# Last stage of a two-layer scan and expert kernel: norms of two chunks loaded with the first chunk's, and third expert layers three pairs behind the first two

## The chip, the cores and the metric

The kernel runs on one core of one Trainium2 chip. The metric is the device time of one execution in microseconds. The time of the kernel before is the median of three runs. A separate execution was recorded by the profiler; it gives the span and the trace, and its times are counted from the start of its span.

## The reference, cut to what matters

A tensor x of 2 batches, 256 channels and 64 x 64 positions goes through a first state-space block, a second bidirectional one, and a soft mixture of 8 experts. The change touches the mixture alone:

```python
def _L1_ffn_ref(x, Wr, br, W1, b1, g1, be1, m1, v1, W2, b2, g2, be2, m2, v2, Wo, bo):
    feat = jnp.mean(x, axis=0)                       # over the two batches
    w = jax.nn.softmax(feat @ Wr + br, axis=-1)      # per position, over 8 experts
    h = jax.nn.relu(_bn(jnp.einsum('bfd,edh->bfeh', x, W1) + b1, g1, be1, m1, v1))
    h = jax.nn.relu(_bn(jnp.einsum('bfeh,ehk->bfek', h, W2) + b2, g2, be2, m2, v2))
    y = jnp.einsum('bfeh,ehd->bfed', h, Wo) + bo
    return jnp.einsum('bfed,fe->bfd', y, w)

t = t + _L1_ffn_ref(_ln_t(t), ...)                   # t: 2 batches x 4096 positions x 256
```

## The kernel before, in words

Channels lie on the 128 partitions, in KC = 2 halves; the 4096 positions are cut into 8 chunks of T = 512. All is float32. A tile of a chunk is 128 x 1024, 512 KB.

A long first stage runs the scans of both state-space blocks for both batches. Beside them it computes as many experts as fit, for 74 of the 128 combinations of batch, chunk and expert. Of these it stores the third layer's product, not yet weighted by the softmax, in DRAM (`u_dram`). It also stores most normalised chunks in `nf_dram`.

The last stage, which the change touches, does the remaining 54 combinations, called pairs here, and sums everything up. Chunk 7 is done for all experts in both batches (`whole`). Chunks 6 to 0 (`rest`, in this order) have batch 1 left: 6 experts of chunk 6, and 8 experts each of chunks 5 to 0.

The steps for a chunk i, with the names by which the trace lists them:

- `load_n` loads the norms n of both batches (L1086, two DMAs of 512 KB in the queue of GpSimd).
- `both` adds the batches to nm on GpSimd (L1108); `logits` multiplies it by Wr on TensorE (lt, L1115) and takes the softmax over experts on VectorE (L1120 to L1134) with an exponential on ScalarE (L1130).
- `spread` transposes the softmax on TensorE (wt, L1140), copies it on ScalarE (wts, L1142), writes it to DRAM (w_dram, L1144) and reads it back to all partitions (wb, L1146, 2048 KB). Both DMAs are in GpSimd's queue. wb has two buffers.
- `load_x` loads the residual x of both batches (L1156, in SP's queue); `bias` multiplies the softmax by bo on TensorE (bi, L1163), copies it on ScalarE (L1164) and adds it to both x on GpSimd (L1166).
- `add_early` loads one early product u (L1170, SP's queue, three buffers), multiplies it by its weight (L1171) and adds it to x (L1172), both on VectorE.
- `layer` computes the first and the second layer of a pair: for each half two products on TensorE (hp, L1201), then a relu with scale and offset on ScalarE (h, L1205). `weigh` multiplies the second layer's h by the softmax weight on VectorE (L1212). `last_layer` adds the third layer's products to y in PSUM (L1220); after the chunk's last pair VectorE adds y to x (L1225) and `store` writes x out (L1175, SP's queue).

The loop over the pairs gives the order of the work, and no scheduler changes it: `in_order` chains each engine's instructions in the order in which they were emitted. In a pair's turn come its weights' loads, its two layers, the weighting of the pair before it, the third layer of the pair two before it, and then a share of the chunk's `side` work. The list `side` of a chunk interleaves its own sums with the routes (`load_n` to `spread`) of a chunk to come, and for chunk 6 with those of chunks 7 and 5; chunk 5's list also has chunk 7's sums. Chunk 6's side work begins in its third pair's turn. As each queue is in order, a waiting instruction holds what stands behind it in its queue.

Of the kernel before, what the change touches and what calls it, by code (L numbers as in the profile page):

```python
# [42 lines left out]
F32 = mybir.dt.float32  # L43
# [4 lines left out]
P = 128  # L48
NB, C, L = 2, 256, 4096
KC = C // P  # L50
T = 512
# [80 lines left out]
def hybrid_kernel(ctx: ExitStack, tc: tile.TileContext, a: dict, out: bass.AP):  # L132
# [49 lines left out]
    def over_channels(t):  # L182
        return t.rearrange("p (o t) -> p o t", o=1).to_broadcast([P, KC, T])


    with ExitStack() as st:
# [121 lines left out]
        )  # L308
        kinds = [(l0, 256, 0, False), (lf, 512, 1, False), (lb, 512, 1, True)]
        jobs = [Scan(p, d, b, layer, flip) for b in range(NB) for p, d, layer, flip in kinds]  # L310
        steps = [(job, c) for job in jobs for c in range(NCH)]
        starts = [sum(8 * job.nj for job, _ in steps[:i]) for i in range(len(steps) + 1)]
# [698 lines left out]
        for g in range(nq):  # L1011
            i, jp, n = quads[g]
# [49 lines left out]
    with ExitStack() as st:  # L1062
        mw = st.enter_context(tc.tile_pool(name="mw", bufs=1))
        mk = st.enter_context(tc.tile_pool(name="mk", bufs=2))
# [3 lines left out]
        n, x, y, acc, wts, wb, lt, w_dram = {}, {}, {}, {}, {}, {}, {}, {}  # L1068
# [5 lines left out]
        rest, whole = [], []  # L1074
# [2 lines left out]

        def load_n(i):

            for b in range(NB):  # L1080
                n[b, i] = mk.tile([P, KC, T], F32, tag="n", name=f"n_{i}{b}", bufs=6)
                if (b, i) in featured:
                    src = nf_dram[b][:, i, :, :]
                else:
                    src = t_dram[b][:, :, i * T : (i + 1) * T]
                nc.gpsimd.dma_start(n[b, i], src)  # L1086

        def layer_norm(i):
            for b in range(NB):
                if (b, i) in featured:  # L1090
                    continue
                v = n[b, i]
                mean = psp.tile([P, T], F32, tag="ps", name=f"mean_m{i}{b}")
                for k in range(KC):
                    nc.tensor.matmul(mean, mean_w, v[:, k, :], start=(k == 0), stop=(k == KC - 1))
                nc.vector.tensor_tensor(v, v, over_channels(mean), ALU.subtract)
                sq = mk.tile([P, KC, T], F32, tag="u", name=f"sq_{i}{b}", bufs=3)
                nc.scalar.activation(sq, v, AF.Square)
                var = psp.tile([P, T], F32, tag="ps", name=f"var_m{i}{b}")
                for k in range(KC):  # L1100
                    nc.tensor.matmul(var, mean_w, sq[:, k, :], start=(k == 0), stop=(k == KC - 1))
                r = mk.tile([P, T], F32, tag="r", name=f"r_{i}{b}", bufs=1)
                rsqrt(r, var, eps5)
                nc.vector.tensor_tensor(v, v, over_channels(r), ALU.mult)

        def both(i):
            n["sum", i] = mk.tile([P, KC, T], F32, tag="nm", name=f"nm_{i}", bufs=1)
            nc.gpsimd.tensor_tensor(n["sum", i], n[0, i], n[1, i], ALU.add)  # L1108

        def logits(i):  # L1110

            lt = psp.tile([P, q, E], F32, tag="ps", name=f"lt_{i}")
            for t in range(q):
                for k in range(KC):
                    nc.tensor.matmul(  # L1115
                        lt[:, t, :], n["sum", i][:, k, t * P : (t + 1) * P], wr[:, k, :],
                        start=(k == 0), stop=(k == KC - 1),
                    )
            w = n["w", i] = mk.tile([P, q, E], F32, tag="w", name=f"w_{i}")
            nc.vector.tensor_tensor(  # L1120
                w, lt, br.rearrange("p (o e) -> p o e", o=1).to_broadcast([P, q, E]), ALU.add
            )
            mx = mk.tile([P, q], F32, tag="mx", name=f"mx_{i}")
            nc.vector.tensor_reduce(mx, w, AX.X, ALU.max)

            def over_experts(v):
                return v.rearrange("p (q o) -> p q o", o=1).to_broadcast([P, q, E])

            nc.vector.tensor_tensor(w, w, over_experts(mx), ALU.subtract)
            nc.scalar.activation(w, w, AF.Exp)  # L1130
            sm = mk.tile([P, q], F32, tag="sm", name=f"sm_{i}")
            nc.vector.tensor_reduce(sm, w, AX.X, ALU.add)
            nc.vector.reciprocal(sm, sm)
            nc.vector.tensor_tensor(w, w, over_experts(sm), ALU.mult)  # L1134

        def spread(i):

            pt = psp.tile([P, T], F32, tag="ps", name=f"wt_{i}")
            for t in range(q):
                nc.tensor.transpose(pt[:E, t * P : (t + 1) * P], n["w", i][:, t, :], ident)  # L1140
            wts[i] = mk.tile([E, T], F32, tag="wt", name=f"wts_{i}", bufs=3)
            nc.scalar.copy(wts[i], pt[:E, :])  # L1142
            w_dram = drp.tile([E, T], F32, name=f"w_dram{i}")
            nc.gpsimd.dma_start(w_dram, wts[i])  # L1144
            wb[i] = mk.tile([P, E, T], F32, tag="wb", name=f"wb_{i}")
            nc.gpsimd.dma_start(  # L1146
                wb[i], w_dram.rearrange("e (o t) -> o e t", o=1).to_broadcast([P, E, T])
            )

        def routes(i):  # L1150
            return [lambda: load_n(i), lambda: layer_norm(i), lambda: both(i), lambda: logits(i), lambda: spread(i)]
# [40 lines left out]
        def load_w(name, e):  # L1192
            we[name, e] = mw.tile([P, KC, C], F32, name=f"{name}_{e}")
            nc.sync.dma_start(we[name, e], a[name][e].rearrange("(k p) n -> p k n", p=P))

        def layer(x, l, e, tag):
            h = mk.tile([P, KC, T], F32, tag=f"h{l}", name=f"h{l}_{tag}", bufs=2 + l)
            for m in range(KC):
                ps = psp.tile([P, T], F32, tag="ps", name=f"hp{l}_{tag}_{m}")
                for k in range(KC):  # L1200
                    nc.tensor.matmul(  # L1201
                        ps, we[f"W{l + 1}", e][:, k, m * P : (m + 1) * P], x[:, k, :],
                        start=(k == 0), stop=(k == KC - 1),
                    )
                nc.scalar.activation(  # L1205
                    h[:, m, :], ps, AF.Relu,
                    bias=of[:, l, e, m : m + 1], scale=sc[:, l, e, m : m + 1],
                )
            return h

        def weigh(b, i, e, h):
            nc.vector.tensor_tensor(h, h, over_channels(wb[i][:, e, :]), ALU.mult)  # L1212

        def last_layer(b, i, e, h):
            begins, ends = (e == [p[2] for p in pairs if p[:2] == (b, i)][k] for k in (0, -1))
            if begins:
                y[b, i] = ps_o.tile([P, KC, T], F32, tag="y", name=f"y_{i}{b}")
            for m in range(KC):
                for k in range(KC):
                    nc.tensor.matmul(  # L1220
                        y[b, i][:, m, :], we["Wo", e][:, k, m * P : (m + 1) * P], h[:, k, :],
                        start=(begins and k == 0), stop=(ends and k == KC - 1),
                    )
            if ends:
                nc.vector.tensor_tensor(x[b, i], y[b, i], x[b, i], ALU.add)  # L1225
                store(b, i)
# [8 lines left out]
        for at, i in enumerate(rest):  # L1235
# [9 lines left out]
            while now or ahead:  # L1245
                work += ahead[:1] + now[:every]
                ahead, now = ahead[1:], now[every:]

        load_n(rest[0])
        for name, e in [("W1", order[0]), ("W2", order[0]), ("W1", order[1]), ("W2", order[1])]:  # L1250
            load_w(name, e)
        nc.sync.dma_start(bo, a["bo"])
        layer_norm(rest[0])
        both(rest[0])
        weights = [("Wo", order[0])]
        for k in range(2, E):
            weights += [("W1", order[k]), ("W2", order[k]), ("Wo", order[k - 1])]
# [2 lines left out]
        waiting = []  # L1260
        done = {i: 0 for i in rest}
        count = {i: sum(p[1] == i for p in pairs) for i in rest}
        for at, (b, i, e) in enumerate(pairs):
            for name, k in weights[: 6 if at else 4]:
                load_w(name, k)
            weights = weights[6 if at else 4 :]
            h = layer(n[b, i], 0, e, f"{i}_{e}_{b}")
            h = layer(h, 1, e, f"{i}_{e}_{b}")
            if at == 0:
                logits(i)  # L1270
            elif at == 1:
                spread(i)
            if waiting:
                weigh(*waiting[-1])
            waiting.append((b, i, e, h))
            if len(waiting) > 2:
                last_layer(*waiting.pop(0))
            done[i] += 1
            work = side[i] if at > 1 else []
            upto = -(-len(work) // (count[i] - done[i] + 1))  # L1280
            for fn in work[:upto]:
                fn()
            side[i] = side[i][upto:]
# [107 lines left out]
```

## Time and profile before

| what | value |
|---|---|
| median of 3 runs | 5206.82 us (5206.63 to 5207.61) |
| the profiled execution | 5213.06 us |
| its span | 5211.3 us |
| busy: PE (TensorE), DVE (VectorE), ACT (ScalarE), POOL (GpSimd) | 4298.0, 4584.8, 3681.8, 4410.2 us |
| last product of the first stage ends | 4541.8 us |
| first hp product of the last stage | 4555.17 us |
| first hp product of chunk 4 | 4748.47 us |
| busy in the last stage's L1201, L1220 on PE | 408.3, 198.0 us |
| idle before them | 15.8, 14.5 us |

PE, DVE, ACT and POOL are the four computing engines; SPq is the queue of SyncE, which only issues DMAs here. A row of the timeline gives the start in us, the duration, the engine, the line, the operation, the tiles written and read, their shapes, how many instructions the row merges, and in brackets the engine's idle time before it with what ended it. Each float32 product of the program shows as two matmul records. A row of the chain of waits gives start, duration and work: the chain is followed back from the last instruction, at each step to what released it. A row of stretches gives the stretch and its length, then busy us and number of instructions for PE, the weight loads PEld, DVE, ACT and POOL, then the granted clock of TensorE as a share of full speed, the mean busy share of the 16 DMA engines, and GB/s.

### The profile page before, as it was taken

What the parts mean: (1) busy time and instruction counts of PE and PEld (TensorE: products, weight loads), DVE (VectorE), ACT (ScalarE), POOL (GpSimd) and SP (SyncE); (2) the same over time, 40 slices, a digit from 0 to 9 for tenths busy, and PEclk for the clock granted to TensorE, in tenths of its full rate; (3) what the DMA queues carried; (4) which work ended last, traced back from release to release, by engine and by line L of the source; (5) the groups of instructions that cost most, each with busy time, mean ns of one, the idle gap of its engine ahead of it and who ended that gap; (6) DMA issues with size and microseconds to landing.
All of it is one profiled execution on the core that took longest, in us unless ns stands there. A gap on an engine that the chain in (4) does not pass through costs nothing. (4 is left out here: it accounts for less than half of the span.)

```text
span 5211.3 us, 47295 instructions
## 1 busy us (share of the span) xinstructions
PE 4298.0 (82%) x14920; PEld 1488.2 (29%) x14920; DVE 4584.8 (88%) x3083; ACT 3681.8 (71%) x7462; POOL 4410.2 (85%) x1438
## 2 busy tenths in 40 slices
PE   5777666766668888888888888888999989689999
PEld 1222212222222333332222332322333333234444
DVE  6998999999999999998989999999999999746333
ACT  5777777777767888887887888788788888522332
POOL 5998999999999999998989999999999999611010
PEclk8778888888889999999999999999999999899999
DMA  4444433344434554555555544445544455354322
GB/s 175 146 165 164 162 134 126 130 156 148 140 135 159 187 186 166 181 174 185 197 177 182 178 169 169 164 159 194 184 171 163 163 184 178 115 194 154 111 103 77
DMA packets 314731, 834.47 MB, mean 160 GB/s; under 512 B 35240, under 2 KB 102064, under 8 KB 272496
## 3 DMA queue, kind: packets, MB, share of 16 engines
q1 hardware_dynamic: 310768, 806.15, 44.5%
q0 software_dynamic: 3712, 25.30, 1.2%
q8 instruction: 118, 1.93, 0.1%
q14 instruction: 133, 1.09, 0.1%
HBM read 647.18 MB, written 184.16 MB: 160 GB/s over the span
## 5 line engine op out<-in xcount | busy, mean ns | idle before, releaser
L654 POOL TENSOR_TENSOR bq<-rxdt,bc 128x2048 f32<-128x2048 f32 x640 | 2892.9, 4542 | 34.8 <-issue 17.4
L664 ACT ACTIVATE da<-rdt,w_a 128x512 f32<-128x512 f32 x2560 | 1756.8, 686 | 113.6 <-DVE bq L690 67.8
L690 DVE TENSOR_TENSOR_SCAN da<-da,h_state,bq 128x1024 f32<-128x1024 f32 x664 | 1559.5, 2349 | 38.7 <-ACT da L664 27.3
L715 POOL TENSOR_TENSOR bq<-bq,bc 128x2048 f32<-128x2048 f32 (+1 forms) x280 | 1179.6, 4213 | 22.5
L723 PE MATMUL y<-bq,stack 128*32 128x512 f32 x5120 | 779.4, 687 | 362.1 <-POOL bq L715 337.2
L690 DVE TENSOR_TENSOR_SCAN bq<-da,h_state,bq 128x1024 f32<-128x1024 f32 x456 | 1052.3, 2337 | 27.9 <-ACT da L664 27.8
L699 DVE TENSOR_TENSOR bq<-da,bc 128x1024 f32<-128x1024 f32 x760 | 928.2, 1221 | 18.7
L912 PE MATMUL e<-eh,ew 128*128 128x512 f32 x1184 | 582.4, 621 | 60.5 <-DVE sp L513 20.5
L709 ACT COPY h_state<-da 128x2 f32<-128x2 f32 x759 | 119.3, 157 | 687.5 <-DVE bq L699 685.4
L675 ACT ACTIVATE bq<-h_state,bq,a 128x1 f32<-128x1 f32 x1120 | 429.9, 384 | 0.5
L723 PEld LDWEIGHTS y<-bq,stack 128*32 128x32 f32 x5120 | 144.9, 118 | 935.1 <-POOL bq L715 458.6
L1205 ACT ACTIVATE h<-hp,of,sc 128x512 f32<-128x512 f32 x216 | 167.7, 777 | 345.0 <-PE hp L1201 328.5
L414 PE MATMUL xs<-nx,w_in 128*128 128x512 f32 x640 | 320.1, 630 | 36.8 <-DVE xc L466 20.7
L414 PE MATMUL z<-nx,w_in 128*128 128x512 f32 x640 | 326.2, 638 | 23.7 <-DVE sp L513 16.9
L912 PEld LDWEIGHTS e<-eh,ew 128*128 128x128 f32 x1184 | 212.4, 193 | 422.3 <-issue 194.5
L912 PE MATMUL e<-en,ew 128*128 128x512 f32 x592 | 290.5, 622 | 47.3 <-DVE fcen L809 21.5
L452 PE MATMUL conv<-xs,w_conv 64*64 64x512 f32 x2560 | 320.5, 608 | 4.6 <-DVE sp L513 3.7
L761 PE MATMUL o<-sz,w_out 128*128 128x512 f32 x640 | 306.7, 620 | 0.0
L923 ACT ACTIVATE eh<-e,of,sc 128x512 f32<-128x512 f32 x296 | 223.7, 769 | 37.9 <-PE e L912 36.7
L517 POOL TENSOR_TENSOR xdt<-sp,xc 128x512 f32<-128x512 f32 x160 | 203.4, 1275 | 53.3 <-DVE sp L513 53.3
L501 PE MATMUL dt<-dbc,w_dt 64*128 64x512 f32 x320 | 197.2, 701 | 44.5 <-ACT dbc L488 27.7
L730 PE MATMUL y<-xc,w_d 128*128 128x512 f32 x320 | 181.0, 649 | 60.8 <-DVE sz L742 51.3
(138 smaller groups left out, 5043.0 us busy)
## 6 DMA issues: line engine op xcount, KB each, us to landing
rxdt<-xdtd SPq DMA_DIRECT2D x160, 1024.0 KB, 6.4
rdt<-dtd SPq DMA_DIRECT2D x160, 1024.0 KB, 6.3
bc<-bcd SPq DMA_DIRECT2D x384, 256.0 KB, 3.2
dtd<-sp SPq DMA_DIRECT2D x160, 256.0 KB, 3.5
xdtd<-xdt SPq DMA_DIRECT2D x160, 256.0 KB, 3.4
ew<-in_W SPq DMA_DIRECT2D x148, 256.0 KB, 4.8
u<-eu SPq DMA_DIRECT2D x74, 512.0 KB, 3.5
u<-u SPq DMA_DIRECT2D x74, 512.0 KB, 4.0
```

Source lines behind the costliest of these rows:

```text
L414: nc.tensor.matmul(ps, job.w["in", half][:, k, j * P : (j + 1) * P], rhs, start=(k == 0), stop=(k == KC - 1),)
L452: nc.tensor.matmul(v[r][64 * col : 64 * col + 64, :], job.w["conv"][rows, 2 * jp + j, k, :], ck["xs", jp][rows, j, k : k + T] if k < 4 els ...
L654: nc.gpsimd.tensor_tensor(bq[g], ck["rxdt", j], over_groups(ck["bc", 0, sg]), ALU.mult)
L664: nc.scalar.activation(da[g, h][:, k, :], cks[i]["rdt", j][:, q, :], AF.Exp, scale=steps[i][0].w["a"][:, j, q * SG + sg : q * SG + sg + 1],)
L675: nc.scalar.activation(bq[g][:, q, 0:1], job.h[:, j, sg, q : q + 1], AF.Identity, scale=cks[i]["a0", j][:, h, sg : sg + 1], bias=bq[g][:, ...
L690: nc.vector.tensor_tensor_scan(b if on_pool(g, h) else d, d, b, job.h[:, j, sg, 2 * h : 2 * h + 1] if c else 0.0, ALU.mult, ALU.add,)
L699: nc.vector.tensor_tensor(bq[g][:, two, :], d, cks[i]["bc", 1, sg].rearrange("p (o t) -> p o t", o=1).to_broadcast([P, 2, T]), ALU.mult,)
L715: nc.gpsimd.tensor_tensor(b, b, cks[i]["bc", 1, sg].rearrange("p (o t) -> p o t", o=1).to_broadcast([P, groups, T]), ALU.mult,)
L723: nc.tensor.matmul(y[i, j][q * CG : (q + 1) * CG, :], stack, bq[g][:, q, :], start=False, stop=(sg == SG - 1),)
L761: nc.tensor.matmul(v[m], job.w["out"][:, j, m * P : (m + 1) * P], ck["sz", j], start=False, stop=(j == job.nj - 1),)
L912: nc.tensor.matmul(ps, ew[l][:, k, m * P : (m + 1) * P], key[x][:, k, :], start=(k == 0), stop=(k == KC - 1),)
L923: nc.scalar.activation(key[dst][:, m, :], key["ps", l, m], AF.Relu, bias=of[:, l, e, m : m + 1], scale=sc[:, l, e, m : m + 1],)
```

## The change

`load_n` returns at once when a chunk's norms are loaded already. It is called for chunks 7 and 5 ahead of the loop, right after chunk 6's nm; their routes' own calls then do nothing. The second layers' h gets four buffers instead of three. The third layer of a pair is emitted in the turn of the pair three after it, not two. The weighting is left out in the turns of pairs 0 and 1; pair 0's comes in turn 2, those of pairs 1 and 2 in turn 3, and from turn 4 on again that of the pair before. At the end, three third layers are left for after the loop instead of two.

```diff
         def load_n(i):
 
+            if (0, i) in n:
+                return
             for b in range(NB):
                 n[b, i] = mk.tile([P, KC, T], F32, tag="n", name=f"n_{i}{b}", bufs=6)
...
         def layer(x, l, e, tag):
-            h = mk.tile([P, KC, T], F32, tag=f"h{l}", name=f"h{l}_{tag}", bufs=2 + l)
+            h = mk.tile([P, KC, T], F32, tag=f"h{l}", name=f"h{l}_{tag}", bufs=2 + 2 * l)
...
         layer_norm(rest[0])
         both(rest[0])
+        for i in whole[:1] + rest[1:2]:
+            load_n(i)
         weights = [("Wo", order[0])]
...
-            if waiting:
-                weigh(*waiting[-1])
+
+            for p in {0: [], 1: [], 2: waiting[:1], 3: waiting[1:]}.get(at, waiting[-1:]):
+                weigh(*p)
             waiting.append((b, i, e, h))
-            if len(waiting) > 2:
+            if len(waiting) > 3:
                 last_layer(*waiting.pop(0))
```

## The prediction

> **What bounds the kernel now.** I first cut the trace into stretches of time. The last stage's first multiplication starts at 4555.17 us. Up to 4748.47, where chunk 4's first layer begins, TensorE is busy 167 of 193 us; from there to the end it is busy 454.6 of 457.5.
>
> ```profile
> 4555.17:4748.47 193.30, 167.46 (x412) 74.40 (x413) 108.33 (x104) 49.33 (x69) 31.62 (x22) 0.93 0.55 194
> 4748.47:5206.00 457.53, 454.56 (x1086) 195.20 (x1084) 169.96 (x156) 138.79 (x184) 46.05 (x32) 1.00 0.29 103
> ```
>
> So only the first 193 us can be shortened. TensorE's rows in the timeline show each gap there, with its releaser in brackets:
>
> ```profile
> 4588.27 5.79 PE L1220 MATMUL y<-h,Wo 128*128 128x512 f32 x8 [7.61 <-DVE h L1212]
> ...
> 4610.08 1.02 PE L1140 MATMUL wt<-ident,w 128*8 128x128 f32 x4 [1.65 <-DVE w L1134]
> ...
> 4630.33 3.58 PE L1115 MATMUL lt<-wr,nm 128*128 128x8 f32 x16 [7.66 <-POOL nm L1108]
> ...
> 4691.19 5.40 PE L1220 MATMUL y<-h,Wo 128*128 128x512 f32 x8 [3.64 <-DVE h L1212]
> ...
> 4707.01 3.70 PE L1220 MATMUL y<-h,Wo 128*128 128x512 f32 x8 [3.28 <-DVE h L1212]
> ...
> 4741.06 3.70 PE L1201 MATMUL hp<-h,W 128*128 128x512 f32 x8 [1.87 <-ACT h L1205]
> ```
>
> The gaps are 25.7 us together. The blocks after them are also longer than an undisturbed one: 5.79 against 3.60, 1.02 + 4.64 against 0.60 + 3.60, 3.58 + 5.22 against 1.85 + 3.60, 5.40 and 3.70 against 3.60, 8.9 us in all. The prize is 34.6 us.
>
> The third view is the chain of waits. From 4659 to 4741 TensorE isn't on it. VectorE adds the early experts' products, and in between the queue SP waits for a finished output before it starts the next loads:
>
> ```profile
> 4690.02 0.39 SPq L1175
> 4690.47 5.59 DMA u<-u
> 4696.08 1.24 DVE u L1171
> ...
> 4715.31 1.23 DVE x L1172
> 4716.56 0.39 SPq L1175
> ...
> 4718.44 6.22 DMA u<-u
> 4724.68 3.26 DVE u L1171
> ...
> 4738.31 1.23 DVE x L1172
> 4740.25 0.77 ACT h L1205
> ```
>
> The reader should see a second bound close behind the gaps: this serial chain, not TensorE, decides when 4741 comes.
>
> **What the Trainium skill says.** "PSUM — Partial Sum Buffer", Engine vs sequencer instructions: the queues of ScalarE, VectorE and GpSimd are strict FIFO. The trace agrees: GpSimd's nm of chunk 7 (4601.29) follows its bias adds (4596.67), and ScalarE's layer at 4740.25 sits behind the softmax's exponential at 4740.12. "SBUF — State Buffer", SBUF: two separate sides: a VectorE operation with two SBUF inputs and a GpSimd one take a shared port in turn, each for its whole length. It agrees: L1172 takes 3.36 us at 4599.05 beside GpSimd, 1.22 alone. "DMA: Bandwidth & Descriptors", Issuing engines are not separate DMA queues: SP's and GpSimd's transfers share the same 16 engines, so loading earlier moves traffic and adds no bandwidth. "TensorE: Matmul & The Clock Gate", Part 1: idleness lowers the array's clock, about 3.4 us of work restores it; the longer blocks above agree roughly (3.64 us idle cost 1.8, 3.28 cost 0.1).
>
> **The change, part by part.** Call chunk 6's pairs p0 to p5 and chunk 5's q0 to q7. Undisturbed steps from start to start, by the timeline: first layer 3.43 (3.5 after lt or bi), second 3.71, y 3.43, lt 1.70, wt 0.43, bi 1.91.
>
> *Two chunks' norms early.* Four 512 KB loads go into GpSimd's queue after nm of chunk 6, so at 4557.6; chunk 7's were issued at 4578.1 and chunk 5's at 4614.65. Their issue (4 x 0.54) fills idle GpSimd time before w_dram at 4574.63, and the later issues go. They compete with the weights: 2.1 MB at the 321 GB/s of 4555 to 4588 is 6.5 us of traffic, but half of it ran beside wb (4577.60 to 4586.97) before. The weights of p0 to p2 were issued earlier than the loads; those of p3 have until 4582. Bounds for wb's landing: the fastest landing of a wb is 8.2 against 9.4, so -1 us, and +6.5 if all 2.1 MB stand ahead of w_dram. I take 0, since one 1 MB load leaves its company as another enters. Benefit: the lt of chunk 5 no longer waits at 4630.33 (7.66 and 3.3 of slow blocks).
>
> *Third layers three behind.* No instruction is added; one more h buffer is held. p0's y now stands behind p3's layers. p0 to p2 end at 4580.5, bi ends at 4582.4, p3 at 4589.6. wb lands at 4587.0; p0's weighting then overlaps GpSimd's bias adds and nm (bi start + 2.68, for 8 us, thus 4583.2 to 4591.2) and takes some 3.4: about 4590.4. The 7.6 us gap becomes 0.8. Behind that weighting on VectorE stand u_0's add, p1's and p2's weighting and the softmax: 4590.4 + 0.8 + 1.2 + 2.3 gives about 4595. lt of chunk 7 runs 4593.9 to 4595.6, its softmax starts at 4595.8, so the wt gap stays (1.7, and 1.4 slow).
>
> From there: wt 4597.4, p4 4598.2, p1's y 4602.7 + 3.7 = 4606.4, lt of chunk 5 4609.8 (nm: GpSimd after wb's issue at 4601.4, by 4605, in time), p5 4611.5. VectorE's softmax comes about a microsecond late and holds ScalarE 0.4. wt 4622.5, q0 **4622.9**; before, 4646.4. Then p3's y and bi of chunk 7 at **4633.5** (before 4657.08).
>
> VectorE after p4: u_7 ends 4620.4, the output and loads cost 5.5 as before (4641.44 to 4646.91), two adds and p5's weighting end about 4632. That releases chunk 5's wb, queued on GpSimd ahead of the bias adds; it lands near 4643. The bias adds start 2.68 after bi, 4636.2, and before q0's weighting there are 10.44 us as before (4659.76 to 4670.20): **4646.6**.
>
> *What moves on VectorE and SP.* x += y of chunk 6 (L1225) and its store stood before u_3 of chunk 7; SP's loads queued behind that store, and VectorE idled 5.37 (ending 4677.93). Now both come after u_7. There SP waits for that output anyway: u_3 to u_7 and q1's weighting run without a stall, 4647.8 to 4661; y of chunk 6 ended at 4656.7; x += y ends at 4662.1, SP's two outputs and a load cost 6.5, first add of batch 1 **4668.6** (before 4696.08: 27.5 earlier). Everything from there to chunk 4's softmax is one chain and keeps this 27.5: u_7 4689, output, loads of chunk 5's x (4694.7 for its bias add), exponential 4740.12 - 27.5 = **4712.7**, q7's second layer 4713.6.
>
> TensorE without waiting: q3's y at 4697.5 ends at 4701.0; lt waits for nm until 4702.7 and ends 4704.5, q7's first layer 4708. It is then idle 5.6 us: the gap of 1.87 has grown, because it is behind VectorE's chain. A gap of that length costs some 1.6 more (between the 0.1 and 2.2 seen). q7's second layer, q4's y, wt; chunk 4 begins at 4721.0 + 1.6 = **4722.6**, 25.9 earlier. But at this point one y fewer has been done: 3.43 comes back later. Net 22.4.
>
> *The rest.* From chunk 4 on there are 8 or 10 adds per 87 us of TensorE work, so VectorE catches up: chunk 5's last y ends 4755, its store and the load follow, first add about 4761, some 13 us later against TensorE than before, against which each y has gained 10.57 of slack; VectorE, busy 56 of 130 us in this chunk before, makes up the rest within it.  At the end three y follow one another after the last layer instead of two; the last weighting (2 us) is hidden, and TensorE's total is equal. I cost these at 0 (0 to 3 if the softmax of chunk 3 is reached late).
>
> Sum: 22.4 us of the profiled execution, 5213.1 (span 5211.3) to 5190.7. The median of the runs is 6.2 below the profiled one, and nothing suggests that those 6 us lie in this stage: 5206.8 - 22.4 = **5184**.
>
> **Rivals.**
> *A, TensorE paces:* the loads or outputs on SP cost less and VectorE's chain isn't the last. Left are 0.8 and 3.1 of gaps: 34.6 - 3.9 = 30.7, **5176**. For it: VectorE is busy only 108 of 193. Against: three SP round trips in series remain.
> *B, wb late:* w_dram and wb stand behind the early loads in GpSimd's queue: +6.5 for everything after p3, and a cold restart of 2.2: 13.7 gained, **5193**. For it: those engines were 91% busy from 4555 to 4588. Against: a dip to 45 GB/s at 4577.
> *C, no change:* VectorE's chain after bi takes up the lead (its adds wait for bi and SP, not for norms): **5203**. Against: the chain begins with TensorE's bi, which comes 23.6 earlier.
> *D, slower:* VectorE begins its adds earlier, beside more traffic, and its u loads have three buffers. A load is hidden while it lands within two adds, 4.8 us; the median is 4.4 and the longest 9.3. 29 adds lie before chunk 4's softmax; if each three wait for a 9.3 landing, 29/3 x 4.5 = 43.5 are lost: 5206.8 - 22.4 + 43.5 = **5228**. It decides from 7.1 us on (29/3 x 2.3 = 22.4). Against: after 4588 the DMA share is 0.33 to 0.55.
>
> **Chances.** Forecast 0.64, A 0.13, B 0.13, C 0.06, D 0.04. The range, 5175 to 5195, takes in A and B with their bounds and leaves C and D out. A measurement of this kernel tells about 0.2%, 10 us, from no change. Faster: forecast, A and nearly all of B, 0.88; same: C and the rest of B, 0.08; slower: D, 0.04.
>
> **What would show it.** Right: no gap at lt of chunk 5; p0's y waits under 2 us; the wt gap stays; q0's first layer about 67.8 us after the stage's first multiplication (before 91.2); a gap of 4 to 7 us before q7's second layer, behind chunk 4's exponential; none after. Wrong: wb landing over 3 us later after its issue; VectorE waiting over 7 us for any u; gaps after chunk 4 begins.

## The result and the profile after

The changed kernel takes 5189.31 us in the median of 6 runs (5187.39 to 5190.60), the kernel before 5207.22 (6 runs): ratio 0.9963, 95% interval 0.9951 to 0.9974, or 13.5 to 25.5 us. The forecast was 5184, the range 5175 to 5195. One of the later runs of the kernel before took 6108 us at a granted clock of 0.658 against some 0.92 in all others; it is left out of every figure.

The profiled execution has a span of 5188.1 us. In its `kernel.py` the lines of the last stage stand two lower, so hp is L1203, y L1222, u and x L1173 and L1174, the store L1177. First the two stretches again, each from the start of the same operation as before; the second goes to 5188.00 here, where the span ends, and went to 5206.00 of 5211.3 before:

```profile
4552.65:4721.86 169.21, 162.83 (x405) 72.14 (x405) 109.76 (x105) 49.11 (x69) 31.58 (x22) 0.94 0.63 222
4721.86:5188.00 466.14, 458.00 (x1094) 196.72 (x1092) 161.49 (x155) 138.72 (x184) 43.12 (x32) 1.00 0.29 102
```

The first stretch went from 193.3 to 169.2 us and TensorE's idle time in it from 26 to 6. It did 7 fewer matmul records there by this trace and has 8 more in the second stretch: one pair's y, which has moved behind this point. Taken to the end of the span, the second stretch grew by that y alone, from 462.8 to 466.2 us. From the first product to the end of the span the last stage took 656.1 us before (5211.3 - 4555.17) and takes 635.4 now (5188.1 - 4552.65): **20.7 us less**. I call this the stage's length and use it below, because the first stage, which no edit touches, varies by as much as some of the edits bring.

TensorE's gaps in the timeline, with the blocks behind them:

```profile
4595.09 1.02 PE L1142 MATMUL wt<-ident,w 128*8 128x128 f32 x4 [2.38 <-DVE w L1136]
4595.90 5.95 PE L1203 MATMUL hp<-n,W 128*128 128x512 f32 x8
...
4614.81 3.70 PE L1203 MATMUL hp<-h,W 128*128 128x512 f32 x8 [0.60 <-ACT h L1207]
...
4701.88 2.57 PE L1117 MATMUL lt<-wr,nm 128*128 128x8 f32 x16 [1.24 <-POOL nm L1110]
4704.29 6.43 PE L1203 MATMUL hp<-n,W 128*128 128x512 f32 x8
4712.75 5.40 PE L1203 MATMUL hp<-h,W 128*128 128x512 f32 x8 [2.03 <-ACT h L1207]
```

The reader should see which rows of before have no successor here: no y waits any more (7.61, 3.64 and 3.28 before), and the lt of chunk 5 doesn't wait for nm (7.66). The wt gap stayed. The end of the stretch, at lt of chunk 4 and q7's second layer, now waits more than before. The chain of waits says for what:

```profile
4661.50 0.39 SPq L1177
...
4661.94 0.46 SPq L1177
...
4662.45 5.46 DMA u<-u
4667.93 1.24 DVE u L1173
...
4688.41 0.39 SPq L1177
...
4690.29 6.08 DMA u<-u
4696.39 3.23 DVE u L1173
...
4711.94 0.77 ACT h L1207
4712.75 5.40 PE hp L1203 x8
```

It is the chain that was shown for before, its first add after the store (4667.93) 1.9 us later in the stage than forecast: finished output, SP's store, the loads queued behind it, VectorE's adds, the softmax, ScalarE, TensorE.

### The profile page after: what moved, and what is told of

Its sections match the earlier page's. It is cut to its first block, busy times and chain, and to the rows that moved or that the text cites. A ratio compares the mean times of both kernels' runs of the same rounds, so it can differ in the third digit from the quotient of the medians.

```text
span 5188.1 us, 47283 instructions
## 1 busy us (share of the span) xinstructions
PE 4301.2 (83%) x14920; PEld 1485.8 (29%) x14920; DVE 4576.1 (88%) x3083; ACT 3681.7 (71%) x7462; POOL 4407.2 (85%) x1438
```

## The experiments

The stages' lengths, each from its own trace (span less the start of the first hp product). The fifth column ends where chunk 4's first layer begins, the sixth is explained below:

| kernel | first product | span | stage | to chunk 4 | var_m and layer |
|---|---|---|---|---|---|
| before | 4555.17 | 5211.3 | 656.1 | 193.30 | 7.01 |
| before, second trace | 4557.17 | 5212.0 | 654.8 | 192.02 | 6.95 |
| changed | 4552.65 | 5188.1 | 635.4 | 169.21 | 6.95 |
| loads alone | 4554.39 | 5200.4 | 646.0 | 184.82 | 5.38 |
| lag alone | 4548.95 | 5195.5 | 646.6 | 182.00 | 5.38 |
| later stores | 4549.42 | 5175.2 | 625.8 | 160.05 | 6.94 |
| later transpose | 4554.37 | 5188.7 | 634.3 | 168.02 | 6.95 |
| both of these | 4559.62 | 5182.4 | 622.8 | 158.53 | 5.37 |
| weighting as before | 4548.16 | 5181.6 | 633.4 | 168.85 | 5.37 |
| chunk 5's loads alone | 4551.22 | 5186.1 | 634.9 | 168.62 | 6.95 |

The last column is one place far behind the start of chunk 4: var_m, TensorE's product for the variance in the norms of one late chunk, and the first layer after it, from var_m's start to the start of the second layer. TensorE waits 2.40 us before it in all ten traces, and yet the two blocks took 5.4 us in four of them and 6.9 to 7.0 in six. These are the rows of the changed kernel and of "weighting as before":

```profile
5016.27 3.05 PE L1103 MATMUL var_m<-sq,mean_w 128*128 128x512 f32 x4 [2.40 <-ACT sq L1100]
5019.12 4.26 PE L1203 MATMUL hp<-n,W 128*128 128x512 f32 x8
```

```profile
5011.43 1.98 PE L1103 MATMUL var_m<-sq,mean_w 128*128 128x512 f32 x4 [2.40 <-ACT sq L1100]
5013.25 3.60 PE L1203 MATMUL hp<-n,W 128*128 128x512 f32 x8
```

The granted clock over these blocks was 0.75 in the first and 1.00 in the second. This difference of 1.6 us doesn't follow the edits (the kernel before and the changed kernel both have the long blocks), and it is in the stage's length; so where an edit is worth only a few us, the column to chunk 4 says more. Each kernel but the one before has one trace, and that one's two traces differ by 1.3 us to chunk 4.

**Early loads alone.** From the kernel before:

```diff
         def load_n(i):
+            if (0, i) in n:
+                return
...
+        for i in whole[:1] + rest[1:2]:
+            load_n(i)
         weights = [("Wo", order[0])]
```

> Early loads alone, third layers two behind as before. Theory (the two halves take away different gaps, so they add up): the first y still waits for wb, 7 to 9 us plus 2 of slow blocks, the lt of chunk 5 no longer waits for nm (11 us with its slow blocks), chunk 4's first layer begins some 10 us earlier after the stage's first product than before (183 instead of 193.3): 5197. Rival (the early loads do everything, the lag nothing): 5189. Rival (the loads push wb back and give nothing by themselves): 5207.

Measured: ratio 0.9983 (0.9976 to 0.9990), 5201.9 against 5211.2 of the kernel before on the same chip; the stage is 10.1 us shorter than before, 8.5 of it ahead of chunk 4, which begins 184.8 us after the first product. TensorE's gaps at y in this kernel's timeline:

```profile
4588.31 5.40 PE L1222 MATMUL y<-h,Wo 128*128 128x512 f32 x8 [8.42 <-DVE h L1214]
...
4681.40 6.63 PE L1222 MATMUL y<-h,Wo 128*128 128x512 f32 x8 [3.78 <-DVE h L1214]
...
4697.89 5.23 PE L1222 MATMUL y<-h,Wo 128*128 128x512 f32 x8 [2.71 <-DVE h L1214]
```

All three waits at y are still there; lt of chunk 5 runs without one. The loads alone give roughly half.

**Third layers three behind alone.** The changed kernel less its two lines ahead of the loop:

```diff
-        for i in whole[:1] + rest[1:2]:
-            load_n(i)
```

> Third layers three behind alone, norms of chunks 7 and 5 loaded where they were. Theory: no gap at the first y, but lt of chunk 5 waits some 9 us for nm, because its loads stand behind wb of chunk 7; VectorE's u_3 no longer waits behind a store. Chunk 4 begins about 180 us after the first product, of which 3.4 come back at the end: 5197. Rival (the lag does everything): 5189. Rival (the gap only moves from y to lt): 5205.

Measured: ratio 0.9982 (0.9973 to 0.9990), 5200.9 against 5211.2; stage 9.6 us shorter than before. TensorE's two largest gaps:

```profile
4612.73 3.58 PE L1117 MATMUL lt<-wr,nm 128*128 128x8 f32 x16 [7.49 <-POOL nm L1110]
...
4720.48 6.77 PE L1203 MATMUL hp<-h,W 128*128 128x512 f32 x8 [5.40 <-ACT h L1207]
```

No y waits; lt of chunk 5 waits 7.49, where I had expected 9. The two halves, 10.1 + 9.6 = 19.7, nearly make up the 20.7 of both, but both halves' traces had the short blocks at var_m. Up to chunk 4 they save 8.5 and, less the 3.4 of the y that comes back, 7.9: together 16.4 against 20.7. So each half takes away its own gaps and is worth some 8 us, and neither rival holds; that the two just add up, as I had expected, one trace of each doesn't show. The fourth h buffer wasn't tried by itself. Before the change ScalarE, which fills these buffers, waits up to chunk 4 only for TensorE's hp and once for a weight load, so there was no wait for a buffer that it could have removed.

**Later stores.** In the changed kernel a finished output's store is put into SP's queue only after three more u have been asked for:

```diff
             nc.sync.dma_start(u, u_dram[b, i, e])
+            for s in list(late):
+                s[0] -= 1
+                if s[0] == 0:
+                    put_out(*s[1:])
+                    late.remove(s)
...
-        def store(b, i):
+        late = []
+
+        def put_out(b, i):
             nc.sync.dma_start(
...
+        def store(b, i):
+            late.append([3, b, i])
...
         for p in waiting:
             last_layer(*p)
+        for s in late:
+            put_out(*s[1:])
```

> The changed kernel, with each finished output stored only after three more loads of u have been issued on SP. Theory (what is left before chunk 4 is VectorE's chain, held by SP waiting at finished outputs): VectorE's waits of 5.7, 6.5 and 5.7 us for u shrink, chunk 4's softmax comes some 11 us earlier, and TensorE's two gaps at lt and q7's second layer (1.2 and 2.0) go with their slow blocks (some 5): 8 us off, 5181. Rival (the chain is bound by VectorE's own adds and the bias of chunk 7): 5188 to 5189.

Measured: ratio 0.9946 (0.9933 to 0.9958) to the kernel before; stage 625.8, 9.7 us less than the changed kernel, 9.2 of it ahead of chunk 4. The ratio's interval overlaps that of the changed kernel (0.9951 to 0.9974), so it is the traces that tell the two apart. VectorE's idle times in this kernel's timeline (its lines are moved again: u, x at L1178, L1179):

```profile
4623.02 1.23 DVE L1178 TENSOR_TENSOR u<-u,wb 128x1024 f32<-128x1024 f32 x1 [0.91 <-DMA u<-u]
4634.14 3.36 DVE L1179 TENSOR_TENSOR x<-x,u 128x1024 f32<-128x1024 f32 x1 [9.89 <-POOL x L1168]
...
4698.55 0.19 DVE L1122 TENSOR_TENSOR w<-lt,br 128x32 f32<-128x32 f32 x1 [1.07 <-PE lt L1117]
```

The changed kernel's waits of 5.74, 6.46 and 5.74 us for u behind a store are gone; VectorE waits 0.53 for a u of chunk 6 and 0.91 for chunk 7's first. The first of the three was worth nothing by itself: VectorE now waits 9.89 instead of 4.32 for the bias adds of chunk 7, which begin with TensorE's bi. The other two were the chain. In the last row VectorE waits for TensorE's lt, the other way round from before, and TensorE has no gap in chunk 5 any more. So the second bound is the wait of the loads behind the stores on SP.

**Later transpose.** In the changed kernel chunk 7's whole `spread` (the transpose wt, its copy and the DMAs w_dram and wb) comes behind nm of chunk 5 in the routes' list, and so behind p4's layers and p1's y:

```diff
                 ahead += routes(j)
+            if not at:
+                ahead.insert(7, ahead.pop(4))
```

> The changed kernel, with the transpose of chunk 7's softmax moved behind p4's layers and p1's y, and nm of chunk 5 put ahead of it. Theory: the gap of 2.4 us at wt and the slow blocks behind it (2.8) go, bi of chunk 7 comes 5 us earlier, VectorE follows by some 4 until its last add of chunk 6 is the limit: 5185. Rival (VectorE's chain sets the time and doesn't begin with bi): 5189. Rival (later wb of chunk 7 holds VectorE): above 5190.

Measured: ratio 0.9959 (0.9946 to 0.9971) to before; stage 634.3, only 1.1 us less than the changed kernel, where I had expected some 4. TensorE's gaps:

```profile
4590.47 3.70 PE L1222 MATMUL y<-h,Wo 128*128 128x512 f32 x8 [1.46 <-DVE h L1214]
...
4613.95 3.70 PE L1203 MATMUL hp<-h,W 128*128 128x512 f32 x8 [1.76 <-ACT h L1207]
...
4702.41 2.02 PE L1117 MATMUL lt<-wr,nm 128*128 128x8 f32 x16 [2.62 <-POOL nm L1110]
...
4713.29 5.40 PE L1203 MATMUL hp<-h,W 128*128 128x512 f32 x8 [3.70 <-ACT h L1207]
```

The wt gap and its slow block are gone, and chunk 7's bi came 2.6 us earlier (77.7 against 80.2 after the first product) and not 5. Of the two new gaps only the 1.76 comes with the edit. The 1.46 stands ahead of the first operation that was moved, and the later stores' trace, with chunk 7's transpose where it was, has 1.45 there. What differs is which of two operations started first: in the changed kernel p0's weighting on VectorE started at 4585.44, GpSimd's nm of chunk 7 at 4585.56, and the weighting took 1.24 us; with the later stores nm started at 4582.37, the weighting at 4582.41, and it took 3.38. In this trace nm is ahead as well (4586.99 and 4587.43), and the weighting took 2.99.

Of the 2.6 us chunk 4 kept 1.2 (168.02 against 169.21): VectorE lost 0.91 waiting for a u at 4647.29, and the gaps at the end of its chain grew (2.62 and 3.70 against 1.24 and 2.03). That fits a TensorE which doesn't pace the end of the changed kernel's chunk 5.

**Both together.** The two edits above in one kernel.

> The changed kernel with both the later stores and the later transpose of chunk 7's softmax. Theory (with the stores moved, TensorE paces the stage, so what the transpose saves TensorE is no longer lost to VectorE's chain): last stage, from its first product to the end of the span, 623.5 us against 625.8 with the stores alone and 635.4 of the changed kernel; about 5178. Rival (VectorE's early adds take the saving again): 625.8, and the same time as the stores alone.

Measured: 5175.54 against 5210.49 of the kernel before on the same chip, ratio 0.9934 (0.9920 to 0.9948); stage 622.8, 3.0 less than with the stores alone. Only half of the 3.0 is the transpose's: chunk 7's bi comes 1.5 us earlier than with the stores alone (78.14 against 79.66 after the first product), chunk 4 as well (158.53 against 160.05), and the rest is var_m's shorter blocks. So with the stores out of the way all that TensorE saves at wt is kept, but the expected stage, 623.5, was met with help of chance. Of TensorE's gaps these two are left before chunk 4:

```profile
4596.20 3.70 PE L1232 MATMUL y<-h,Wo 128*128 128x512 f32 x8 [1.46 <-DVE h L1224]
...
4619.68 3.70 PE L1213 MATMUL hp<-h,W 128*128 128x512 f32 x8 [1.75 <-ACT h L1217]
```

This version has the lowest time of all: its ratio's interval lies below that of the changed kernel's (0.9951 to 0.9974), but overlaps that of the later stores alone (0.9933 to 0.9958).

**Weighting as before.** The changed kernel with the turns' special cases undone:

```diff
-            for p in {0: [], 1: [], 2: waiting[:1], 3: waiting[1:]}.get(at, waiting[-1:]):
-                weigh(*p)
+            if waiting:
+                weigh(*waiting[-1])
```

> The changed kernel with each pair weighted in the turn after its own from the start, as before the change; the lag of three and the early loads stay. Theory: VectorE has the same operations before chunk 7's softmax, p1's weighting only stands ahead of u_0's add; last stage 635 to 636, no gap over 2 us at the first y. Rival (delaying the weightings to turns 2 and 3 is what frees the first turns): a gap of some 3 us or more again, 638 or more.

Measured: ratio 0.9960 (0.9945 to 0.9974); stage 633.4, and no gap at the first y. The wt gap is 2.74 and the one at q7 3.70. The stage is 2.0 shorter than the changed kernel's, outside the 635 to 636 expected, but only 0.4 of it lies ahead of chunk 4; the rest is var_m's shorter blocks. So I don't read a gain from it; delaying the first weightings isn't what frees the turns, the lag does that.

**Chunk 5's loads alone early.**

```diff
-        for i in whole[:1] + rest[1:2]:
+        for i in rest[1:2]:
             load_n(i)
```

> The changed kernel with chunk 5's norms alone loaded early; chunk 7's are loaded behind chunk 6's wb, as before the change. Theory (chunk 7's nm waits for the bias adds ahead of it on GpSimd and not for its load): the gain stays but for 0 to 3 us, nm of chunk 7 waiting up to 1.5 us for its load as in the run without early loads; last stage 635 to 638. Rival (chunk 7's early load is half of the gain of the loads): 640 or more.

Measured: ratio 0.9956 (0.9942 to 0.9971); stage 634.9, as with both. Here GpSimd's nm of chunk 7 does wait for its load, 2.92 us where up to 1.5 was expected; in its timeline:

```profile
4586.97 3.06 POOL L1110 TENSOR_TENSOR nm<-n,n 128x1024 f32<-128x1024 f32 x1 [2.92 <-DMA n<-nf_dram]
```

and lt of chunk 7 waits 0.60 us for it. Chunk 4 comes no later for it (168.62 us against 169.21). The gain of the loads is chunk 5's.

**The kernel before once more.**

> The kernel before once more, for a second trace. Theory (the difference between what the last stage lost, 20.7 us, and the difference of the medians is the first stage, which varies from execution to execution by some us and which the change doesn't touch): last stage 655 to 657 again, the stage's first product anywhere from 4549 to 4557. Rival (the last stage itself varies by as much): last stage under 653 or over 659.

Measured: stage 654.8, first product at 4557.17, each 0.2 outside what I had written, and far from the rival's bounds. Over the ten traces of the table the first product lies between 4548.2 and 4559.6 us, although nothing ahead of it differs. That is how a stage that is 20.7 us shorter (19.4 against this second trace) can show as 17.9 between two medians and as 23.2 between two spans.

## Why the prediction held, step by step

In us after the stage's first product, as predicted and as measured:

| step | predicted | measured |
|---|---|---|
| p0's weighting starts (wb is there) | 31.8 | 32.8 |
| wt of chunk 7 | 42.2 | 42.4 |
| lt of chunk 5 | 54.6 | 56.2 |
| q0's first layer | 67.7 | 69.6 |
| bi of chunk 7 | 78.3 | 80.2 |
| first add of chunk 7's batch 1 | 113.4 | 115.3 |
| q7's second layer | 158.4 | 160.1 |
| chunk 4's first layer | 167.4 | 169.2 |

*The mechanism was right:* both halves, the order of the chain, the wt gap that stays and the y that comes back later (24.1 - 3.4 = 20.7). *One size was off.* The error of 1.8 us at chunk 4 arises between wt of chunk 7 and q0, in the term "1.4 slow" behind the wt gap: wt and the first layer there took 1.02 + 5.95 against 0.60 + 3.60, so 2.8. The gap itself was 2.38 instead of 1.7, ScalarE held 0.6 instead of 0.4, and against these the first y didn't wait at all where I had put 0.8. That was luck: p0's weighting started 0.12 us ahead of GpSimd's nm and took 1.24 us instead of my 3.4; three other traces have the wait, 1.45 or 1.46. Later steps add nothing; the chain carried the 1.8 to its end. The median lies 5.3 above the forecast, and these 1.8 are less than that: the rest isn't traced, and the first product's place alone varies by 11 us.

*Early loads beside wb:* taken at 0, bounded by -1 and 6.5; wb was there 1.0 later. The pieces changed more than their sum. In GpSimd's timeline:

```profile
4572.31 0.52 POOL L1146 DMA_DIRECT2D w_dram<-wts  x1 [15.18 <-ACT wts L1144]
4578.47 0.53 POOL L1148 DMA_DIRECT2D wb<-w_dram  x1 [5.65 <-DMA u<-u]
```

From w_dram's issue to wb's it is 6.2 us (before 3.0), and from wb's issue to p0's weighting 7.0 (before 9.4), less than the 8.2 that I had taken as the fastest. The second row names a u that landed at about the same time; w_dram, which wb must wait for, landed 5.9 us after its issue (before 2.7). The reason that I gave, one load leaving wb's company as another enters, was therefore not what happened, and that the sum came out near 0 was luck. Nor is all of it the early loads' doing: with the lag alone, the norms loaded behind wb as before, it was 4.6 and 7.4. As the prediction had it, no bandwidth was added: from 4555 to 4588 the DMA engines moved 329 GB/s, before 324. Rival B priced the same place at 6.5 and didn't come.

*The end of the chain:* I put 1.7 of wait at lt, 5.6 of idleness at q7 and 1.6 of slow work, 8.9 together. It was 1.24 and 2.03 idle, and 0.7, 2.8 and 1.7 in slower blocks, 8.5. The sum was nearly right, again by pieces that made up for one another; less of it is seen as idleness, because TensorE ran at a lower rate through lt and q7's first layer (granted clock 0.74 from 4701.80 to 4704.30, 0.57 from there to 4710.80). My sign "a gap of 4 to 7 us" was wrong in this form.

*The rivals.* A (TensorE paces) needed the stores moved as well: only then is TensorE the one that is waited for, and the stage is 30.3 us shorter than before, close to the 30.7 that A had priced. C and D didn't occur; the longest of VectorE's waits for u is 6.46, behind a store, not for landing alone. One u did land late, 10.9 us after its issue beside chunk 7's wb; it cost VectorE 2.85 (at 4610.79) and, through chunk 5's softmax and ScalarE, TensorE the 0.60.

After chunk 4 begins no gap but the 2.4 us before var_m is left in either kernel, and only the y's 3.4 us came back there.

## What to carry to other kernels

SP's queue here carries both stores and loads fetched ahead, and a store that waited for its result delayed every load behind it; putting it three loads later took 9.2 us off up to chunk 4, with no instruction more. Look for the same in other in-order queues. Before pricing the gaps of the busiest engine, follow the chain of waits through the place where they are: if another engine's chain is close behind, only that part of a saving is kept which the chain can follow, as the later transpose showed (1.2 of 2.6 us alone, 1.5 of 1.5 with the chain out of the way). Compare small edits by the length of their own stage when the stages ahead vary more than the edit, and end that length where the edit's effect ends: a single gap behind it varied by 1.6 us.

## What the runs showed of the hardware

The cost of a gap on TensorE didn't follow its length. Before var_m the same 2.40 us cost nothing in four traces and 1.6 us in six. At y, among waits under 4 us, those of 1.45, 2.29 and 3.28 were followed by a block of 3.70 us, those of 2.71, 3.36 and 3.64 by one of 5.2 to 5.4, and one of 3.78 by 6.63; undisturbed it takes 3.60. At chunk 4's lt, waits of 0.86, 1.24, 1.30 and 2.62 were followed by a first layer of 5.1 to 6.4, and one of 1.58 by 3.68. At chunk 7's wt the gaps of 1.65 to 2.74 were all followed by a first layer of 4.6 to 6.2.

The Trainium skill, "TensorE: Matmul & The Clock Gate", What's actually happening, says that the activity is judged in a free-running window of about 3.4 us, and puts the lower rate at half. That such a cost depends on where the gap falls agrees with these rows, var_m's above all. An estimate from these two figures, one window at half rate, is a loss of 1.7 us. It fits var_m's 1.6, three rows at y, three at lt and three at wt, each with the layer behind it (1.5 to 1.8). It doesn't fit the 3.0 lost at y after 3.78, the changed kernel's lt with its layer (3.5), or the other five rows at wt (2.6 to 3.0). That the lt ahead of wt, whose 16 records have 8 columns each, counts with the gap would fit the wt rows, but no run separates it.

A 16 KB write to DRAM (w_dram) held the DMA that reads it back for 2.1 us (chunk 7's wb in the changed kernel) to 6.2 us (chunk 6's). What else was in flight is the likely reason, but no run was made to show it.
